# One VectorE instruction for both rows of a sum, and a scratch tile with its channel chunks interleaved by fours

## The chip, the cores and the metric

The kernel runs on one core of a Trainium2 chip. A core has a TensorE (PE) for matrix products, a VectorE (DVE) and a ScalarE (ACT) for elementwise work, a GpSimd (POOL), and a SyncE (SP) that here only issues DMA transfers. The engines run side by side, each through its own list of instructions in order, and wait for each other through semaphores. SBUF is the working memory (128 partitions), PSUM takes what PE writes. The metric is the device time of one execution in microseconds (us), lower is better. Before the change the median of three runs is 2844.78 us (2844.46 to 2845.08).

## The reference

The input `x` has 4 images of 64 channels of 256 x 256 in float32. Four layers follow each other. Layers 0, 1 and 3 are long convolutions with a separable filter per channel (the reference does them by FFT; the filters come from small networks with sines), plus `x * bias`. Layer 2 is the one that the change touches: a two-dimensional Haar transform, two branches that each scale the coefficients, mix the 64 channels and soft-threshold the result, their sum, the inverse transform, and a residual.

```python
f1 = haar2d(x)
acc = jnp.zeros_like(f1[:, :conv_w.shape[1]])
for i in range(v.shape[0]):                       # two branches
    f3 = f1 * v[i]
    f4 = jnp.einsum('bchw,oc->bohw', f3, conv_w[i])
    f5 = jnp.sign(f4) * jax.nn.relu(jnp.abs(f4) - tau[i])
    acc = acc + f5
y = haar2d(acc, inverse=True)
return y + x
```

## The kernel before, in words

**Convolutions** (`convolutions`, `first`, `second`, `contract`). Each image goes channel by channel through layers 0 and 1. A convolution is two products on PE with Toeplitz tiles (L286, L287); ACT copies the first product out of PSUM (L300), VectorE adds the residual to the second (L317). Then VectorE, ACT, POOL and PE do the forward Haar transform: pairs (L366, L367), levels along the row (L379, L380), a split of a number into two parts (L398 on ACT, L403 on VectorE) and a product with a Haar matrix (L410). The coefficients go to DRAM.

**Mixing** (`mixing`, 64 groups `g` per image). A group is two rows of coefficients, with all 64 channels. PE mixes the channels (`mix`, L480): `px` in PSUM holds 16 columns of 64 output channels: two branches, two rows `q`, and two halves of each row with two columns. The products with `v` are made by VectorE for the first `16 - n_act` columns (`scaled`, L502, one instruction per four columns) and by ACT for the others (`scaled_too`, L507). `n_act` is 12 for the first three images and 8 for the last (`N_ACT`), so VectorE has one such instruction per group in the first three mixings and two in the last. ACT then makes the absolute value (`size`, L511) and the sign (`sign`, L514); VectorE subtracts the threshold (`shrink`, L518) and makes max(., 0) times sign (`signed`, L522), 1024 elements each. Last, `add` (L528) sums the two branches into the two rows of `z` to which the group belongs, one instruction of 256 elements per row.

**The tile z.** `z` holds a whole image of the mixed coefficients: 128 partitions with 32,768 numbers each, as `[128, 4, 128, 4, 16]`: a chunk `n` of 16 channels, a row `s`, four column parts `x`, and the channel `c` within the chunk. A row's place is given by `slot`, in such a way that each later step of the inverse transform works in place.

**Inverse** (`inverse`). The inverse Haar transform down the rows is done in `z` on VectorE, by `halve`: `odd = even - odd` (L326) and `even = 2 * even - odd` (L329). `butterfly` does it for the first rows; `level(n, chunk, begin, count)` does it for `count` pairs of rows of one chunk (64 elements per row, 4 column parts by 16 channels). For n of 1, 2, 4, 8, 16, 32 and 64 these have up to 16 pairs at a time, so up to 1024 elements. Then, channel by channel, ACT copies one channel out of `z` (`fetch`, L569: 128 rows by 4 column parts, 512 elements far apart), PE applies the other direction (`rows`, L576 and L577; `halves` and `cols` for some channels), VectorE joins it with the residual (L598, L601, L602), and layer 3 follows as the convolutions did. A part of the channels of the first three images (`put_off`) has its layer 3 in the last mixing (`convolution`).

**Order.** Every step is entered with a time of its own (`at`, in units of one channel or group, from `PLACE` and `LATE`), and the steps are emitted in order of these times; a scheduler then settles each engine's list. The convolutions of the next image lie beside the mixing of the one before it. The first filters, their tables and a few constants are put into `z` before it is used (`room`, `part`).

Of the kernel before, what the change touches and what calls it, by code (L numbers as in the profile page):

```python
# [9 lines left out]
F32 = mybir.dt.float32  # L10
F32R = mybir.dt.float32r
AF = mybir.ActivationFunctionType
ALU = mybir.AluOpType
# [3 lines left out]
B, C, S, EMB, ORD = 4, 64, 256, 33, 64  # L17
P = 128
# [92 lines left out]
def conv_seq_kernel(ctx, tc, x, fz, fw, bias, decay, haar, haar_row, factors, vt, taut, wmix, out):  # L111
# [14 lines left out]
    nc = tc.nc  # L126
# [5 lines left out]
    zpool = ctx.enter_context(tc.tile_pool(name="zpool", bufs=1))  # L132
# [13 lines left out]
    bsb = const.tile([P, 3, C], F32, name="bsb")  # L146


    z = zpool.tile([P, 4, P, 4, 16], F32, name="z")

    sd = zpool.tile([P, 8, 2, 2, P], F32, name="sd")
    sums = zpool.tile([P, 4, 2, P], F32, name="sums")
# [6 lines left out]

    room = z.rearrange("p n s x c -> p (n s x c)")
    free = [0]

    def part(n, parts=P):
# [158 lines left out]
    def halve(even, odd, stay=False):  # L324

        first = nc.vector.tensor_sub(odd, even, odd)  # L326
        if stay and behind[0] is not None:
            tc.add_manual_dep(first.ins, behind[0].ins.name, order, reason="not ahead of the joins")
        nc.vector.scalar_tensor_tensor(even, even, 2.0, odd, ALU.mult, ALU.subtract)  # L329

    def level(n, chunk, begin=0, count=None, stay=False):

        count = n if count is None else count
        v = z.rearrange("p n s x c -> p n s (x c)")[:, chunk].rearrange("p (j e s) x -> p j e s x", e=2, s=P // 2 // n)
        halve(v[:, begin : begin + count, 0, 0, :], v[:, begin : begin + count, 1, 0, :], stay)

    def butterfly():

        v = z.rearrange("p n s (k h) c -> p n s k h c", k=2)
        for h in range(2):  # L340
            halve(v[:, :, 0, 0, h, :], v[:, :, 0, 1, h, :])

# [3 lines left out]
    def at(time, run, unit):  # L348
        events.append((time, len(events), run, unit))
# [104 lines left out]
    def mixing(b, start, n_act):  # L454

        st = {}

        def load(g):
            f = mx.tile([P, 2, S], F32, name=f"f_{b}_{g}", tag="f", bufs=3)
            nc.sync.dma_start(f, coef[b].rearrange("k c p w -> (k c) p w")[:, 2 * g : 2 * g + 2])  # L460
            st[g] = {"f": f}
            if g % GT == 0:
                t = mx.tile([P, 2, GT, 16], F32, name=f"vt_{b}_{g}", tag="vt")
                nc.sync.dma_start(t, scales[:, g // GT])
                st["vt", g // GT] = t

        def scale(g, i):
            return st["vt", g // GT][:, i, g % GT, :]

        def over(g, i, n):  # L470
            return scale(g, i)[:, :n].unsqueeze(2).to_broadcast([P, n, C])

        def mix(g):
            f = st[g]["f"]
            ps = psx.tile([P, 2, 2, S], F32, name=f"px_{b}_{g}", tag="mix")
            for q in range(2):
                for h in range(2):
                    for r in range(2):
                        half = slice(r * C, (r + 1) * C)
                        nc.tensor.matmul(  # L480
                            ps[:, r, q, h * P : (h + 1) * P],
                            f[half, q, h * P : (h + 1) * P],
                            wb[half],
                            start=True,
                            stop=True,
                        )
            if g == 0:

                one, two = ps[:, 0, 0], ps[:, 1, 0]
                d = mx.tile([P, S], F32, name=f"d_{b}", tag="mag")  # L490
                nc.vector.tensor_copy(d, two)
                nc.vector.tensor_sub(two, one, d)
                nc.vector.tensor_add(one, one, d)
            st[g]["f4"] = mx.tile([P, 16, C], F32, name=f"f4_{b}_{g}", tag="f4")
            st[g]["px"] = ps.rearrange("p r q (h i o) -> p r q (h i) o", h=2, i=2)

        def scaled(g):
            px, n = st[g]["px"], 16 - n_act
            for r in range(n // 4):
                j = slice(4 * r, 4 * r + 4)  # L500
                v = scale(g, 0)[:, j].unsqueeze(2).to_broadcast([P, 4, C])
                nc.vector.tensor_tensor(st[g]["f4"][:, j], px[:, r, 0], v, ALU.mult)  # L502

        def scaled_too(g, half):
            px, f4 = st[g]["px"], st[g]["f4"]
            for j in range(16 - n_act + half * (n_act // 2), 16 - (1 - half) * (n_act - n_act // 2)):
                nc.scalar.mul(f4[:, j], px[:, j // 4 % 2, j // 8, j % 4], scale(g, 0)[:, j : j + 1])  # L507

        def size(g):
            mag = st[g]["mag"] = mx.tile([P, 16, C], F32, name=f"mag_{b}_{g}", tag="mag")  # L510
            nc.scalar.activation(mag, st[g]["f4"], AF.Abs)  # L511

        def sign(g):
            nc.scalar.activation(st[g]["f4"], st[g]["f4"], AF.Sign)  # L514

        def shrink(g):
            mag = st[g]["mag"]
            nc.vector.tensor_sub(mag, mag, over(g, 1, 16))  # L518

        def signed(g):  # L520
            mag = st[g]["mag"]
            nc.vector.scalar_tensor_tensor(mag, mag, 0.0, st[g]["f4"], ALU.max, ALU.mult)  # L522

        def add(g):
            parts = st.pop(g)["mag"].rearrange("p (q x i) (n c) -> p q i x n c", q=2, i=2, n=4)
            for q in range(2):
                to = slot(2 * g + q)
                nc.vector.tensor_add(  # L528
                    z[:, :, to].rearrange("p n x c -> p x n c"), parts[:, q, 0], parts[:, q, 1]
                )  # L530


        for g in range(S // 4):
            for name, stage in zip(
                ("mix load", "mix", "scaled", "scaled too", "scaled rest", "size", "sign", "shrink", "signed", "add"),
                (
                    load,
                    mix,
                    scaled,
                    lambda g: scaled_too(g, 0),  # L540
                    lambda g: scaled_too(g, 1),
                    size,
                    sign,
                    shrink,
                    signed,
                    add,
                ),
            ):
                at(start + g + PLACE[name if b + 1 < B else "l " + name], stage, g)

    def inverse(b, start, put_off):

        st = {}
# [11 lines left out]

        def fetch(c):
            a = mx.tile([P, 2, 2, P], F32, name=f"zc_{b}_{c}", tag="mag")
            v = z[:, c // 16, :, :, c % 16].rearrange("p i (k h) -> p h k i", k=2)
            nc.scalar.copy(a, v)  # L569
            st[c]["z"] = a  # L570

# [38 lines left out]
        def when(tick, n, chunk, *span, stay=False):  # L610
            at(tick + PLACE["level"], lambda _: level(n, chunk, *span, stay=stay), 0)

        at(along + 11 + PLACE["level"], lambda _: butterfly(), 0)
        for chunk in range(1, 4):
            turn = start + 16 * (chunk - 1)
# [14 lines left out]
        for c in range(C):  # L630
            for name, stage in zip(("sooner", "early", "fetch", "rows"), (sooner, early, fetch, rows)):
                at(start + c + PLACE[name], stage, c)
            turn = start + c
            if c < 16:
                at(start + c + PLACE["halves"], halves, c)
                at(start + c + PLACE["cols"], cols, c)
                turn += 1
            at(turn + PLACE["join"], join, c)
            if c in put_off:
                at(turn + PLACE["aside"], aside, c)  # L640
            else:
                shift = (0.0, 0.0)
                if put_off and not {c - 1, c + 1}.issubset(put_off):
                    shift = ((-0.27, -0.342), (0.23, 0.158))[c % 3]
                for name, stage in zip(("a3", "a3 copy", "y3", "y3 sum", "out"), last(b, st)):
                    at(turn + PLACE[name] + shift[name[0] != "a"], stage, c)
# [80 lines left out]
def slot(i):  # L727

    if i == 0:
        return 0  # L730
    n = 1 << i.bit_length() - 1
    return (2 * (i - n) + 1) * (P // 2 // n)
# [104 lines left out]
```

## Time and profile before

The profile is one execution, taken by the hardware profiler. Its span runs from the first to the last instruction; the time of that same execution is a little longer.

| | |
|---|---|
| time, median of 3 runs | 2844.78 us |
| time of the profiled execution | 2842.56 us |
| span of the profiled execution | 2840.7 us |
| PE busy | 2732.7 us (96%), 18642 products |
| PE loading weights | 2438.6 us (86%) |
| VectorE busy | 2494.6 us (88%), 4333 instructions |
| ACT busy | 2077.6 us (73%), 4941 instructions |
| POOL busy | 333.9 us (12%) |
| DMA | 653.20 MB, 230 GB/s |

The page also shows the span in 40 equal slices of 71 us; each digit is the share of a slice in which the engine was busy, in tenths. The clock that TensorE was granted (PEclk) was full throughout.

```profile
PE   9999999999999999999999999999999999899999
DVE  5655558999998979999998879999998889999985
ACT  2333348999986559989886658999985669998554
```

The first six slices are the convolutions of the first image. The four mixings are the stretches in which ACT is at eight or nine; an inverse follows each of them.

### The profile page before, as it was taken

To read this page: it belongs to the slowest core of one execution; us is meant where nothing else is said; L and a number is where in the kernel's file an instruction comes from. 1 tells how busy PE (TensorE), PEld (TensorE's weight loads), DVE (VectorE), ACT (ScalarE), POOL (GpSimd) and SP (SyncE) were. 2 spreads that over 40 slices of the span, in tenths; PEclk is the share of its full clock that TensorE was granted. 3 is DMA by queue.
4 is the path that set the end of the run, shared out by engine and by line. 5 is a ranking of instruction groups with operands and counts; after the bars stand their busy time and mean duration, and the time that the engine had idled before them with its cause. 6 is when DMAs were issued, how large, how long until landed. Compare 5 with 4: busy or idle time off the path is not lost. (4 is left out here: it accounts for less than half of the span.)

```text
span 2840.7 us, 56683 instructions
## 1 busy us (share of the span) xinstructions
PE 2732.7 (96%) x18642; PEld 2438.6 (86%) x18642; DVE 2494.6 (88%) x4333; ACT 2077.6 (73%) x4941; POOL 333.9 (12%) x644
## 2 busy tenths in 40 slices
PE   9999999999999999999999999999999999899999
PEld 8999998888889898888889998888889987787998
DVE  5655558999998979999998879999998889999985
ACT  2333348999986559989886658999985669998554
POOL 0111111121111001212210001312210000000000
PEclk9999999999999999999999999999999999999999
DMA  6877787676667886777677986777778988787786
GB/s 200 258 232 231 227 239 220 209 208 208 206 207 251 287 257 203 211 212 209 205 216 246 292 262 201 210 210 214 208 212 241 296 277 249 234 253 228 227 240 200
DMA packets 597209, 653.20 MB, mean 230 GB/s; under 512 B 44625, under 2 KB 513204, under 8 KB 596660
## 3 DMA queue, kind: packets, MB, share of 16 engines
q1 hardware_dynamic: 545460, 599.82, 70.6%
q10 hardware_dynamic: 51456, 49.75, 5.1%
q8 instruction: 150, 2.46, 0.4%
q14 instruction: 143, 1.17, 0.1%
HBM read 428.34 MB, written 221.05 MB: 229 GB/s over the span
## 5 line engine op out<-in xcount | busy, mean ns | idle before, releaser
L286 PE MATMUL py<-t,a 128*128 128x256 f32 x3072 | 946.3, 390 | 48.7 <-ACT a L300 47.7
L300 ACT COPY a<-pa 128x512 f32<-128x512 f32 x768 | 475.1, 619 | 476.6 <-PE pa L287 448.3
L507 ACT ACTIVATE f<-px,vt 128x64 f32<-128x64 f32 x2816 | 607.6, 354 | 104.2 <-DVE f L502 101.9
L287 PEld LDWEIGHTS py<-t,a 128*128 128x128 f32 x3072 | 583.4, 190 | 79.3
L287 PE MATMUL py<-t,a 128*128 128x128 f32 x3072 | 590.0, 274 | 0.0
L286 PEld LDWEIGHTS py<-t,a 128*128 128x128 f32 x3072 | 479.4, 191 | 112.2 <-ACT a L300 74.6
L380 POOL TENSOR_TENSOR sd<-less 128x128 f32<-128x128 f32 (+4 forms) x320 | 188.5, 589 | 1829.7 <-DVE less L379 1498.1
L286 PE MATMUL pa<-t,y 128*128 128x256 f32 x1024 | 316.5, 391 | 45.0 <-DVE y L317 44.2
L569 ACT COPY zc<-z 128x512 f32<-128x512 f32 x256 | 280.8, 1105 | 104.6 <-PE pw L577 96.7
L518 DVE TENSOR_TENSOR mag<-mag,vt 128x1024 f32<-128x1024 f32 x256 | 316.5, 1236 | 7.5 <-ACT mag L511 6.7
L522 DVE SCALAR_TENSOR_TENSOR mag<-mag,f 128x1024 f32<-128x1024 f32 x256 | 317.4, 1240 | 0.9 <-ACT f L514 0.5
L286 PE MATMUL pa<-t,x 128*128 128x256 f32 x1024 | 308.7, 383 | 0.6 <-DMA pad<-z 0.6
L403 DVE TENSOR_TENSOR sp<-sd,sp 128x512 fp32r<-128x512 f32 x256 | 179.3, 700 | 145.7 <-ACT sp L398 144.3
L480 PE MATMUL px<-wb,f 64*128 64x128 f32 x4096 | 303.7, 285 | 2.2 <-ACT f L507 2.2
L511 ACT ACTIVATE mag<-f 128x1024 f32<-128x1024 f32 x256 | 293.9, 1148 | 5.2 <-DVE z L528 1.2
L514 ACT ACTIVATE f<-f 128x1024 f32<-128x1024 f32 x256 | 283.9, 1109 | 4.1
L480 PEld LDWEIGHTS px<-wb,f 64*128 64x128 f32 x4096 | 252.2, 187 | 36.5 <-ACT f L507 3.0
L317 DVE SCALAR_TENSOR_TENSOR y<-x,bsb,py 128x512 f32<-128x512 f32 x256 | 190.3, 743 | 44.0 <-PE py L287 40.6
L286 PE MATMUL pa<-t,u 128*128 128x256 f32 x748 | 224.6, 382 | 0.7 <-PE pw L577 0.7
L287 PEld LDWEIGHTS pa<-t,y 128*128 128x128 f32 x1024 | 194.5, 190 | 26.4
L287 PEld LDWEIGHTS pa<-t,x 128*128 128x128 f32 x1024 | 194.6, 190 | 26.3
L286 PEld LDWEIGHTS pa<-t,y 128*128 128x128 f32 x1024 | 155.6, 191 | 65.3 <-DVE y L317 62.8
(71 smaller groups left out, 4434.6 us busy)
## 6 DMA issues: line engine op xcount, KB each, us to landing
t<-pad SPq DMA_DIRECT2D x767, 256.0 KB, 4.1
x<-in_x SPq DMA_DIRECT2D x256, 256.0 KB, 3.9
coef<-co SPq DMA_DIRECT2D x256, 256.0 KB, 3.2
f<-coef SPq DMA_DIRECT2D x256, 256.0 KB, 3.5
r<-keep SPq DMA_DIRECT2D x256, 256.0 KB, 4.1
out_y<-y ACTq DMA_DIRECT2D x187, 256.0 KB, 4.2
keep<-sums SPq DMA_DIRECT2D x256, 128.0 KB, 2.8
keep<-sd SPq DMA_DIRECT2D x256, 128.0 KB, 2.7
```

The source lines that it names most:

```text
L286: nc.tensor.matmul(ps[:, m, :], src[:, 0, m * P : (m + 1) * P], t[:, ::-1], start=True, stop=False)
L287: nc.tensor.matmul(ps[:, m, P:], src[:, 1, m * P : (m + 1) * P], t[:, : P - 1 : -1], start=False, stop=True)
L300: nc.scalar.copy(a, s["p" + new])
L317: nc.vector.scalar_tensor_tensor(y, s[res], bsb[:, layer, c : c + 1], s["p" + new], ALU.mult, ALU.add)
L380: engine.tensor_tensor(t[:, :, :, half:length], v[..., 0], v[..., 1], ALU.subtract)
L480: nc.tensor.matmul(ps[:, r, q, h * P : (h + 1) * P], f[half, q, h * P : (h + 1) * P], wb[half], start=True, stop=True,)
L507: nc.scalar.mul(f4[:, j], px[:, j // 4 % 2, j // 8, j % 4], scale(g, 0)[:, j : j + 1])
L511: nc.scalar.activation(mag, st[g]["f4"], AF.Abs)
L514: nc.scalar.activation(st[g]["f4"], st[g]["f4"], AF.Sign)
L518: nc.vector.tensor_sub(mag, mag, over(g, 1, 16))
L522: nc.vector.scalar_tensor_tensor(mag, mag, 0.0, st[g]["f4"], ALU.max, ALU.mult)
L569: nc.scalar.copy(a, v)
```

## The change

`z` becomes `[128, 128, 4, 16, 4]`: row `s`, column part `x`, channel `c` within the chunk, and the chunk `n` innermost. A row of all 64 channels is now 256 neighbouring numbers, and the 64 numbers of one chunk in a row are four numbers (16 bytes) apart. The order of the output channels in the mixing weights `wmix` is permuted on the host to match, so that PE delivers the channels in the order `c`, `n`.

With that, `add` writes both rows of a group by one instruction of 512 elements: the two rows are `step` slots apart. In `scaled`, the two instructions of the last mixing become one of 512 elements. `level`, `butterfly` and `fetch` address the new layout: a level reads and writes with a step of four elements, the butterfly works on 64 neighbours, and the fetch steps 256 elements from row to row where it stepped 64.

```diff
-    z = zpool.tile([P, 4, P, 4, 16], F32, name="z")
+    z = zpool.tile([P, P, 4, 16, 4], F32, name="z")
...
-    room = z.rearrange("p n s x c -> p (n s x c)")
+    room = z.rearrange("p s x c n -> p (s x c n)")
...
         count = n if count is None else count
-        v = z.rearrange("p n s x c -> p n s (x c)")[:, chunk].rearrange("p (j e s) x -> p j e s x", e=2, s=P // 2 // n)
+        v = z.rearrange("p s x c n -> p s (x c) n")[:, :, :, chunk]
+        v = v.rearrange("p (j e s) x -> p j e s x", e=2, s=P // 2 // n)
         halve(v[:, begin : begin + count, 0, 0, :], v[:, begin : begin + count, 1, 0, :], stay)
 
     def butterfly():
 
-        v = z.rearrange("p n s (k h) c -> p n s k h c", k=2)
+        v = z[:, 0].rearrange("p (k h) c n -> p k h (c n)", k=2)
         for h in range(2):
-            halve(v[:, :, 0, 0, h, :], v[:, :, 0, 1, h, :])
+            halve(v[:, 0, h], v[:, 1, h])
...
         def scaled(g):
             px, n = st[g]["px"], 16 - n_act
-            for r in range(n // 4):
-                j = slice(4 * r, 4 * r + 4)
-                v = scale(g, 0)[:, j].unsqueeze(2).to_broadcast([P, 4, C])
-                nc.vector.tensor_tensor(st[g]["f4"][:, j], px[:, r, 0], v, ALU.mult)
+            if n == 4:
+                nc.vector.tensor_tensor(st[g]["f4"][:, :4], px[:, 0, 0], over(g, 0, 4), ALU.mult)
+            else:
+                f4 = st[g]["f4"][:, :8].rearrange("p (r j) o -> p r j o", r=2)
+                v = scale(g, 0)[:, :8].rearrange("p (r j) -> p r j", r=2).unsqueeze(3).to_broadcast([P, 2, 4, C])
+                nc.vector.tensor_tensor(f4, px[:, :, 0], v, ALU.mult)
...
         def add(g):
-            parts = st.pop(g)["mag"].rearrange("p (q x i) (n c) -> p q i x n c", q=2, i=2, n=4)
-            for q in range(2):
-                to = slot(2 * g + q)
-                nc.vector.tensor_add(
-                    z[:, :, to].rearrange("p n x c -> p x n c"), parts[:, q, 0], parts[:, q, 1]
-                )
+            parts = st.pop(g)["mag"].rearrange("p (q x i) o -> p q x i o", q=2, i=2)
+            to, step = slot(2 * g), slot(2 * g + 1) - slot(2 * g)
+            v = z.rearrange("p s x c n -> p s x (c n)")[:, to : to + step + 1 : step]
+            nc.vector.tensor_add(v, parts[:, :, :, 0], parts[:, :, :, 1])
...
         def fetch(c):
             a = mx.tile([P, 2, 2, P], F32, name=f"zc_{b}_{c}", tag="mag")
-            v = z[:, c // 16, :, :, c % 16].rearrange("p i (k h) -> p h k i", k=2)
+            v = z[:, :, :, c % 16, c // 16].rearrange("p i (k h) -> p h k i", k=2)
             nc.scalar.copy(a, v)
             st[c]["z"] = a
...
-        "wmix": lay(g["L2_conv_conv_w"].transpose(2, 0, 1).reshape(C, 2 * C)),
+        "wmix": lay(g["L2_conv_conv_w"].transpose(2, 0, 1).reshape(C, 2, 4, 16).swapaxes(2, 3).reshape(C, 2 * C)),
```

## The prediction

> **What bounds the kernel now.** I read the busy time in 40 slices first, then the same by stage for each engine, then the groups of instructions kept apart by shape, the list of waits, and the order of time inside two mixing groups. The stretches below show PE (with its weight loads), VectorE (DVE), ACT and POOL: one of the first convolutions, one each of a mixing, the inverse after it, the last mixing, and the last inverse.
>
> ```profile
> core 0: us, PE busy (x) PEld busy (x) DVE busy (x) ACT busy (x) POOL busy (x), PEclk, DMA share, GB/s
> 284.10:355.10 71.00, 71.00 (x426) 64.83 (x425) 41.66 (x76) 27.18 (x51) 9.24 (x30) 1.00 0.77 228
> ...
> 710.20:781.20 71.00, 66.47 (x480) 57.98 (x479) 70.32 (x112) 66.70 (x194) 11.25 (x20) 1.00 0.68 206
> ...
> 923.20:994.20 71.00, 70.06 (x463) 63.86 (x463) 66.48 (x130) 42.27 (x53) 0.00 (x0) 1.00 0.90 287
> ...
> 2414.60:2485.60 71.00, 63.20 (x518) 54.78 (x519) 71.00 (x117) 68.78 (x179) 0.00 (x0) 1.00 0.78 234
> ...
> 2627.60:2698.70 71.10, 70.45 (x456) 64.99 (x455) 70.33 (x118) 37.50 (x50) 0.00 (x0) 1.00 0.75 227
> ```
>
> The bound changes by stage. The convolutions and most of an inverse are PE's (71.00 of 71; 70.06). The four mixings (about 440 to 852, 1065 to 1491, 1704 to 2130, 2343 to 2600 us) are VectorE's: 70.32 and 71.00 of 71, while PE idles 4 to 8 us per slice. In the last inverse, up to about 2740 us, both are full. PE's 96% over the whole span hides this. VectorE time in a mixing therefore counts nearly one for one.
>
> The groups that the change touches, and those that price it (mean ns of one in the last column before the bar's idle time):
>
> ```profile
> line engine op names shapes xcount | busy us, mean ns | idle before us <-releasers
> L569 ACT COPY zc<-z 128x512 f32<-128x512 f32 x256 | 280.8, 1105 | 104.6 <-PE pw L577 96.7 <-DVE z L528 2.3
> L528 DVE TENSOR_TENSOR z<-mag 128x256 f32<-128x256 f32 x512 | 205.5, 439 | 0.8
> L398 ACT CAST sp<-sd 128x512 fp32r<-128x512 f32 x256 | 178.3, 696 | 4.2 <-POOL sd L380 4.2
> L502 DVE TENSOR_TENSOR f<-px,vt 128x256 f32<-128x256 f32 x320 | 132.1, 441 | 0.1
> L366 DVE TENSOR_TENSOR sums<-y 128x256 f32<-128x256 f32 x256 | 108.2, 423 | 3.5
> L326 DVE TENSOR_TENSOR z<-z 128x1024 f32<-128x1024 f32 x69 | 84.2, 1225 | 0.3
> L326 DVE TENSOR_TENSOR z<-z 128x512 f32<-128x512 f32 x42 | 28.6, 686 | 0.0
> ```
>
> In order of time, one stretch of VectorE in the first mixing (start, length):
>
> ```profile
> 643.23 0.41 DVE L528 TENSOR_TENSOR z<-mag 128x256 f32<-128x256 f32 x1
> 643.57 0.41 DVE L366 TENSOR_TENSOR sums<-y 128x256 f32<-128x256 f32 x1
> 643.90 0.43 DVE L367 TENSOR_TENSOR sd<-y 128x256 f32<-128x256 f32 x1
> ...
> 647.20 0.68 DVE L403 TENSOR_TENSOR sp<-sd,sp 128x512 fp32r<-128x512 f32 x1
> 647.80 0.75 DVE L528 TENSOR_TENSOR z<-mag 128x256 f32<-128x256 f32 x2
> 648.47 0.74 DVE L317 SCALAR_TENSOR_TENSOR y<-y,bsb,py 128x512 f32<-128x512 f32 x1
> ```
>
> Neighbours overlap, so what an instruction takes from its engine is the distance between starts: 0.34 us for 256 elements (643.23 to 643.57), 0.60 for 512 (647.20 to 647.80), 0.67 for two of 256 (647.80 to 648.47).
>
> **What it removes.** The sums of L528 fall from 512 instructions of 256 to 256 of 512: 256 x (0.67 - 0.60) = 17.9 us. The products of L502 in the last mixing fall from 128 to 64: the nearest 512-wide product from PSUM takes 685 ns (L584), as L403's 700, so 64 x 0.07 = 4.5 us; if it took L317's 0.66 between starts, nothing. Per mixing that is 4.5, 4.5, 4.5 and 9.0 us, all where VectorE is full. In the last mixing ACT is next: 68.78 of 71, so at most 3% of 257 us, 7.6, comes through. Gain: 13.5 + 7.6 = 21 us (14 to 22).
>
> [...]
>
> **What it adds.** No instruction; but the halving steps of `level` (L326 and L329) now read both inputs and write in place with a step of four elements (16 bytes), where 64 neighbours lay side by side. The trace has no such VectorE row. Two rows bound it. Below: a step of two (L366 reads, L601 writes) takes 423 and 423 ns against 421 for L326's unstepped 256, so 0 per element. Above: ACT's copy L569 reads this same z with a step of 64 elements and takes 1105 ns, the plain 512-wide L398 696: 0.80 ns more per element. ACT's plain step is 0.81 (L514's 1109 for 1024 less 696, over 512), so its cost per element doubles. VectorE's plain step is (1225 - 686)/512 = 1.05 ns; doubled, 1.05 more. A gain is excluded, since no row with a step is faster than one without. I take the doubling: in a step of two only one side of the instruction was stepped and each element kept a near neighbour, while L569 is the one row with larger steps, on this very tile, and it pays in full. I keep 0 and 0.80 for the other cases.
>
> [...]
>
> Elements per line of code, from the counts by shape in each stretch (69 of 1024, 42 of 512, and 12 each of 256, 128 and 64, the 8 of the butterfly left out): 97,536; two lines at 1.05 ns give 205 us. By stretch: the first three mixings 15,168, 20,288 and 20,288 elements = 31.9, 42.6 and 42.6 us; the last mixing 2,176 = 4.6; the inverses 9,216, 4,096, 4,096 and 22,208 = 19.4, 8.6, 8.6 and 46.6.
>
> **What of it reaches the end.** Mixings: VectorE idles some 4 us in each from its second slice on (0.2 to 1.1 per slice); 3 each may be swallowed: 117.1 - 9 = 108, and 4.6 in the last, which has no idle time. First inverse: its levels lie in 920 to 980 us, where VectorE has 1.2 us idle and PE none to spare later; it can run behind by about a step of 3.3 us (213 us for 64 channels): of 19.4 I take 12 (0 to 18). Second and third: 8.6 against 5.5 idle in the 60 us around: 3 each (0 to 8). Last inverse: 46.6 from 2600 to 2740, where VectorE idles 2.2 us; less a step of lag, 40 (30 to 45); the PE-bound tail after it can't catch up. Queued behind a slower level on VectorE are the products L502 that ACT's L507 waits for, the sums y of L317 that PE's next product waits for (already 44.2 us of PE's idle time), and the joins.
> Sum: 108 + 4.6 + 12 + 6 + 40 = 171; less 21: +150 us.
>
> **At nothing.** The fetch L569 steps 256 elements instead of 64: both far apart; were it to double again (256 x 0.41 = 105 us) ACT, with 5 us or more of each 20 idle in the inverses, would cover most. The butterfly moves from runs of 16 to plain ones, 221 ns either way. The weights' columns are permuted on the host. In the built program the fetches keep their number of waits on VectorE and ACT, levels wait for VectorE alone as before, and the orders of PE, ACT and SP differ by a handful of neighbours; so no new wait between engines, no DMA moved past another. A merged sum gives the first of its two rows 0.27 us later; that is VectorE's own next work.
>
> **Rivals.** (A) The step costs VectorE nothing, like L366's: only the gain, 2844.8 - 21 = 2824 us, faster. For it: steps of 8 bytes are free here; L569 is another engine. Against: L569. (B) The price is ACT's 0.80 ns: 156 us in all; mixings 89.3 - 9 = 80 and 3.5, inverses 8 + 2 + 30, less 21: +103, or 2948; if the inverses hide all theirs at the full price, 108 + 4.6 - 21 = +92, 2936. Against the latter: both engines are full to 2740 us. (C) Two stepped inputs and a stepped output each pay: 410 us on VectorE, of which by the same shares 342 reach the end, less 21: 3166; no row speaks for it. (D) The gain and a small price cancel: at 0.13 ns per element (21/171 of 1.05) the change turns from gain to loss.
>
> **Numbers.** The profiled execution took 2842.56 us (span 2840.7, 1.9 around it), the median is 2844.78, 2.2 above. Forecast: 2844.8 + 150 = 2995, own range 2955 to 3030 (the bounds above and a merge gain of 14 to 22). Chances: forecast 0.60, B 0.18, A 0.17, C 0.03, D 0.02. The range runs from B to the forecast's upper end, 2900 to 3030, and leaves out A, C and D. A measurement tells 0.2% (6 us) from no change: faster 0.17, same 0.02, slower 0.81.
>
> **What would show it.** L326 at 1024 elements near 2.3 us (1.23 under A, 2.05 under B); the merged sum near 0.69 and 256 of them; L502 at 512 wide near 0.69; VectorE over 99% in the mixings, with these some 30 to 40 us longer each; PE's waits on L317 grown; the last inverse some 40 us longer. Wrong above all if L326 keeps 1225 ns, or if VectorE's time grows by 180 us and the span by far less.

## The result, and the profile after

The changed kernel takes 2982.55 us (median of 4 runs, 2980.48 to 2985.22) against 2844.63 us: slower by 138 us, a ratio of 1.0485 (95% interval 1.0472 to 1.0497). Its profiled execution took 2982.83 us with a span of 2981.0 us, 140 more than before.

First four of the five stages shown before, by engine (columns: the stretch and its length, then the busy time of PE, weight loads, VectorE, ACT and POOL, with the number of instructions). The changed kernel, busy time in 40 slices' width:

```profile
core 0: us, PE busy (x) PEld busy (x) DVE busy (x) ACT busy (x) POOL busy (x), PEclk, DMA share, GB/s
...
710.20:781.20 71.00, 61.88 (x442) 53.01 (x442) 70.86 (x98) 62.37 (x185) 13.24 (x20) 1.00 0.66 193
...
923.20:994.20 71.00, 65.66 (x414) 58.37 (x414) 67.05 (x116) 41.32 (x55) 0.00 (x0) 1.00 0.83 259
...
2556.60:2627.60 71.00, 62.10 (x502) 53.86 (x503) 71.00 (x84) 68.24 (x182) 0.00 (x0) 1.00 0.79 233
...
2769.70:2840.70 71.00, 60.78 (x365) 51.83 (x364) 71.00 (x92) 29.22 (x38) 0.00 (x0) 1.00 0.63 188
```

In the mixing VectorE was full before (70.32 of 71 us) and is full now (70.86), with fewer instructions in a slice (98 for 112), and PE's busy time in it falls from 66.47 to 61.88 us. The inverse was PE's (70.06 of 71); now PE has only 65.66, and in the last inverse 60.78 where it had 70.45: PE waits for VectorE there. The wait itself stands in the page's row of the products that read y, first before, then after (us busy, mean ns, idle time before them and who ended it): PE's wait for the sums y of L317 went from 44.2 to 96.7 us.

```profile
L286 PE MATMUL pa<-t,y 128*128 128x256 f32 x1024 | 316.5, 391 | 45.0 <-DVE y L317 44.2
```

```profile
L286 PE MATMUL pa<-t,y 128*128 128x256 f32 x1024 | 322.5, 397 | 97.5 <-DVE y L317 96.7
```

The groups of the changed kernel, shapes apart (mean ns of one after the busy time). The lines moved by a few: the sum L528 is L531, the products are L501 (256 wide) and L505 (512 wide), the fetch is L570.

```profile
line engine op names shapes xcount | busy us, mean ns | idle before us <-releasers
L329 DVE SCALAR_TENSOR_TENSOR z<-z 128x1024 f32<-128x1024 f32 x69 | 144.1, 2089 | 0.1
L326 DVE TENSOR_TENSOR z<-z 128x1024 f32<-128x1024 f32 x69 | 143.9, 2092 | 0.4
L326 DVE TENSOR_TENSOR z<-z 128x512 f32<-128x512 f32 x42 | 46.8, 1118 | 0.0
...
L570 ACT COPY zc<-z 128x512 f32<-128x512 f32 x256 | 282.9, 1113 | 105.9 <-PE pw L578 93.1 <-DVE y L317 5.7 <-DVE z L531 1.8
L531 DVE TENSOR_TENSOR z<-mag 128x512 f32<-128x512 f32 x256 | 181.1, 707 | 0.8
L505 DVE TENSOR_TENSOR f<-px,vt 128x512 f32<-128x512 f32 x64 | 47.3, 739 | 0.0
```

A level of 1024 elements takes 2092 ns where it took 1225: 0.85 ns more per element. Over the 97,536 elements of two lines that is 166 us in lengths of instructions. The merged sums take 181.1 us where the single ones took 205.5. Both changes are there; VectorE's busy time, which counts the overlap of neighbours once, grew by 131 us (2494.6 to 2625.2) and the span by 140.

Where the time lies, from the order of time in both traces (first and last sum of a mixing, first and last fetch of an inverse; us from the start):

| until | before | after | grown by | in this stage |
|---|---|---|---|---|
| first sum, image 1 | 448.7 | 449.4 | 0.7 | 0.7 |
| last sum, image 1 | 847.3 | 869.8 | 22.5 | 21.8 (mixing) |
| last fetch, image 1 | 1030.7 | 1067.5 | 36.8 | 14.3 (inverse) |
| last sum, image 2 | 1483.8 | 1550.5 | 66.7 | 29.9 (mixing) |
| last fetch, image 2 | 1673.8 | 1745.3 | 71.5 | 4.8 (inverse) |
| last sum, image 3 | 2126.8 | 2226.2 | 99.4 | 27.9 (mixing) |
| last fetch, image 3 | 2317.0 | 2420.7 | 103.7 | 4.3 (inverse) |
| first fetch, image 4 | 2608.3 | 2724.4 | 116.1 | 12.4 (last mixing) |
| last fetch, image 4 | 2824.9 | 2965.2 | 140.3 | 24.2 (last inverse) |

### The profile page after: what moved, and what is told of

Same layout as the page of the kernel before. It is cut to its first block, busy times and chain, and to the rows that moved or that the text cites. A ratio compares the mean times of both kernels' runs of the same rounds, so it can differ in the third digit from the quotient of the medians.

```text
span 2981.0 us, 56301 instructions
## 1 busy us (share of the span) xinstructions
PE 2766.7 (93%) x18642; PEld 2447.7 (82%) x18642; DVE 2625.2 (88%) x4013; ACT 2086.4 (70%) x4941; POOL 357.8 (12%) x644
## 3 DMA queue, kind: packets, MB, share of 16 engines
q14 instruction: 139, 1.14, 0.1%
## 5 line engine op out<-in xcount | busy, mean ns | idle before, releaser
L300 ACT COPY a<-pa 128x512 f32<-128x512 f32 x768 | 473.5, 617 | 533.1 <-PE pa L287 448.2
L510 ACT ACTIVATE f<-px,vt 128x64 f32<-128x64 f32 x2816 | 609.0, 350 | 181.1 <-DVE f L501 170.8
L381 POOL TENSOR_TENSOR sd<-less 128x128 f32<-128x128 f32 (+4 forms) x320 | 205.5, 642 | 1911.9 <-DVE less L380 1460.6
L286 PE MATMUL pa<-t,y 128*128 128x256 f32 x1024 | 322.5, 397 | 97.5 <-DVE y L317 96.7
L570 ACT COPY zc<-z 128x512 f32<-128x512 f32 x256 | 282.9, 1113 | 105.9 <-PE pw L578 93.1
L517 ACT ACTIVATE f<-f 128x1024 f32<-128x1024 f32 x256 | 282.7, 1104 | 4.7
L317 DVE SCALAR_TENSOR_TENSOR y<-x,bsb,py 128x512 f32<-128x512 f32 x256 | 190.9, 746 | 46.5 <-PE py L287 36.6
```

The source lines that it names most:

```text
L286: nc.tensor.matmul(ps[:, m, :], src[:, 0, m * P : (m + 1) * P], t[:, ::-1], start=True, stop=False)
L300: nc.scalar.copy(a, s["p" + new])
L317: nc.vector.scalar_tensor_tensor(y, s[res], bsb[:, layer, c : c + 1], s["p" + new], ALU.mult, ALU.add)
L381: engine.tensor_tensor(t[:, :, :, half:length], v[..., 0], v[..., 1], ALU.subtract)
```

## The experiments

Two questions: is it the step of four in the levels that costs the time, and what became of the VectorE time that the merged instructions save?

**Plain levels with both merges.** The changed kernel with `z` seen as row, chunk, column part, channel by the levels and the fetch.

```diff
-    z = zpool.tile([P, P, 4, 16, 4], F32, name="z")
+    z = zpool.tile([P, P, 4, 4, 16], F32, name="z")
...
-        v = z.rearrange("p s x c n -> p s (x c) n")[:, :, :, chunk]
+        v = z.rearrange("p s n x c -> p s n (x c)")[:, :, chunk]
```

> The changed kernel with the merged sum and the merged products, but the levels and the fetch see a row as chunk, column part, channel, so that a level's 64 numbers are neighbours again. The merged sum still writes its 256 numbers of a row straight on, so they land in other channels than they belong to: that part of the computation is changed. Theory 1 (the step of four in the levels costs all of it): L326 at 1024 elements back from 2092 to about 1225 ns, and the time falls below the kernel before by the merges' gain, 2844.6 - 21 = 2824 us (2822 to 2832). Theory 2 (the merged sum, the new order of instructions or the waits of the new layout cost it): L326 may recover, but the time stays above 2900 us.

Measured: 2843.14 us against 2845.83 for the kernel before on the same chip, ratio 0.9993 (0.9983 to 1.0002). From its groups by shape:

```profile
L531 DVE TENSOR_TENSOR z<-mag 128x512 f32<-128x512 f32 x256 | 176.3, 688 | 0.8
...
L326 DVE TENSOR_TENSOR z<-z 128x1024 f32<-128x1024 f32 x69 | 83.7, 1219 | 0.4
```

With the step away, L326 is back at 1219 ns and all 138 us are gone: theory 1 holds, theory 2 falls. But the 21 us that the merges were to bring did not come.

**The step alone.** The changed layout, with the sum and the products in two instructions as before.

```diff
-            v = z.rearrange("p s x c n -> p s x (c n)")[:, to : to + step + 1 : step]
-            nc.vector.tensor_add(v, parts[:, :, :, 0], parts[:, :, :, 1])
+            for q in range(2):
+                v = z.rearrange("p s x c n -> p s x (c n)")[:, to + q * step]
+                nc.vector.tensor_add(v, parts[:, q, :, 0], parts[:, q, :, 1])
```

> The changed kernel's layout of z with a step of four in the levels, but the sum and the last mixing's products in two instructions each, as before the change. Theory 1: the step's 166 us of VectorE time (97,536 elements, two lines, 0.85 ns) reach the end nearly whole, without the merges' gain: 2982.5 + 17 to 21 = 3000 to 3004 us. Theory 2: the time falls back to about 2845 us.

Measured: 2982.49 us, ratio 1.0479 (1.0461 to 1.0496): the time of the full change, not 17 to 21 more. The step carries the whole loss, and the merges are worth nothing in this layout too, though VectorE is busy 21 us less with them (2625.2 against 2646.4). The step by itself made VectorE 152 us busier (2646.4 for 2494.6).

**A step of two.** The kernel before with the chunks of `z` interleaved by twos.

```diff
-    z = zpool.tile([P, 4, P, 4, 16], F32, name="z")
+    z = zpool.tile([P, 2, P, 4, 16, 2], F32, name="z")
...
+        v = z.rearrange("p m s x c n -> p m s (x c) n")[:, chunk // 2, :, :, chunk % 2]
```

> The kernel before, with z in two halves and the two chunks of a half interleaved by twos: the levels step two elements (8 bytes) on both inputs and the output; sum and products are those of before. Theory 1a (the price sets in between a step of two and a step of four): L326 at 1024 elements stays at 1225 ns, time 2845 us (2840 to 2850). Theory 1b (the price grows in proportion with the step): a third of the price of a step of four, 0.28 ns per element, L326 near 1515 ns, time near 2895 us.

Measured: 2849.52 us, ratio 1.0014 (1.0005 to 1.0024), and L326 at 1024 elements 1220 ns. A step of two on both inputs and the output costs the instruction nothing: 1a. The price sets in between 8 bytes (1220 ns) and 16 (2092 in the changed kernel). The time is 3.7 us longer all the same; in the trace the first three inverses take 2 to 3 us more each, for a reason that was not looked for.

**Steps by themselves.** A probe with no part of the computation; the lines of code first, then its groups by shape.

```python
nc.vector.tensor_sub(outs[:, 0:512:1], big[:, 0:512:1], big[:, 8192:8704:1])                  # L121, then steps of
                                                   # 2 (L122), 3 (L123), 4 (L124), 6 (L125), 8 (L126), 16 (L127)
nc.vector.tensor_sub(outs[:, 0:2048:4], big[:, 0:512:1], big[:, 8192:8704:1])                 # L128: output alone
nc.vector.tensor_sub(outs[:, 0:512:1], big[:, 0:2048:4], big[:, 8192:8704:1])                 # L129: one input
nc.vector.tensor_sub(outs[:, 0:512:1], big[:, 0:2048:4], big[:, 8192:10240:4])                # L130: both inputs
                                                   # L135: both inputs in pairs of neighbours, every four
nc.scalar.copy(oa[:, 0:512], big[:, 0:512:1])      # L136, then steps of 2 (L137), 3 (L138), 4 (L139), 8, 16 (L141)
```

> Not the computation at all, but a probe: VectorE subtractions of 512 elements in SBUF with a step of 1, 2, 3, 4, 6, 8 and 16 elements on both inputs and the output; a step of 4 on the output alone, on one input alone, on both inputs alone; the two-step form with a scalar at a step of 4 and of 1; 1024 and 2048 elements at a step of 4; pairs of neighbours every four; and ACT copies of 512 with a step of 1, 2, 3, 4, 8 and 16 on the input and of 4 on the output; 16 of each. If the price is for each access to another 16 bytes: flat (700 ns) at 1 and 2, in between at 3, about 1120 ns at 4 and the same at 6, 8 and 16; pairs cost nothing. If it grows with the step: 16 far above 4. If only inputs pay, the output alone stays at 700 ns; if three streams share one path, both inputs alone would cost less than all three. ACT: 696 at 1 and 2, 1105 at 4 and beyond.

```profile
L139 ACT COPY oa<-big 128x512 f32<-128x512 f32 x16 | 17.8, 1115 | 0.5
L124 DVE TENSOR_TENSOR outs<-big 128x512 f32<-128x512 f32 x16 | 17.3, 1084 | 0.5
...
L128 DVE TENSOR_TENSOR outs<-big 128x512 f32<-128x512 f32 x16 | 17.1, 1069 | 0.5
...
L130 DVE TENSOR_TENSOR outs<-big 128x512 f32<-128x512 f32 x16 | 17.1, 1068 | 0.5
L129 DVE TENSOR_TENSOR outs<-big 128x512 f32<-128x512 f32 x16 | 17.1, 1066 | 0.5
L127 DVE TENSOR_TENSOR outs<-big 128x512 f32<-128x512 f32 x16 | 16.7, 1045 | 0.6
...
L123 DVE TENSOR_TENSOR outs<-big 128x512 f32<-128x512 f32 x16 | 13.5, 846 | 0.5
L122 DVE TENSOR_TENSOR outs<-big 128x512 f32<-128x512 f32 x16 | 11.1, 693 | 0.5
...
L135 DVE TENSOR_TENSOR outs<-big 128x512 f32<-128x512 f32 x16 | 11.1, 692 | 0.5
L121 DVE TENSOR_TENSOR outs<-big 128x512 f32<-128x512 f32 x16 | 11.0, 688 | 0.5
L137 ACT COPY oa<-big 128x512 f32<-128x512 f32 x16 | 10.6, 661 | 0.5
L136 ACT COPY oa<-big 128x512 f32<-128x512 f32 x16 | 9.9, 619 | 27.1 <-DVE oa L119 26.6
```

Read down the last-but-one number: 688 ns plain, 693 at a step of two, 846 at three, 1084 at four, and no more at sixteen (1045). One stepped stream out of three pays as much as all three (1066 to 1069), the output as much as an input. Pairs of neighbours every four elements cost nothing (692). So in these rows the full price stands where each element is 16 bytes or more from the one before it (four and sixteen elements), and part of it at 12 bytes; on ACT too the price is there at a step of four (1115 ns for 619 plain, 661 at two). This fits the expectation's first case, a price for each access to another 16 bytes; what in the chip makes it, these rows do not show. The size is (1084 - 688)/512 = 0.77 ns per element on VectorE here, 0.85 by length in the kernel, and (1115 - 619)/512 = 0.97 on ACT.

**The same merges with plain levels, computed in full** (the relaid kernel below). `z` as before; instead the products and thresholded terms are laid out as chunk, column, channel, so that one sum covers both rows.

```diff
-            st[g]["f4"] = mx.tile([P, 16, C], F32, name=f"f4_{b}_{g}", tag="f4")
+            st[g]["f4"] = mx.tile([P, 4, 16, 16], F32, name=f"f4_{b}_{g}", tag="f4")
...
+            parts = st.pop(g)["mag"].rearrange("p n (q x i) c -> p n q x i c", q=2, i=2)
+            to, step = slot(2 * g), slot(2 * g + 1) - slot(2 * g)
+            nc.vector.tensor_add(z[:, :, to : to + step + 1 : step], parts[:, :, :, :, 0], parts[:, :, :, :, 1])
```

> The kernel before with z, levels, butterfly and fetch untouched; the products and the thresholded terms are laid out as chunk, column, channel instead, so that the sum of both rows and the last mixing's products are one instruction each without any step in the levels. ACT's products L507 and VectorE's L502 write runs of 16. Theory 1: L326 at 1225 ns, the sum near 0.70 us for 512, time 2824 us (2820 to 2834), faster than both kernels. Rival: runs of 16 cost ACT time on 2816 products; at 20 ns each 56 us, of which the last mixing, where ACT has 2 us idle of 71, would pay 20: about 2840 to 2850 us.

Measured: 2842.93 us, ratio 0.9991 (0.9982 to 1.0000): no loss, and again hardly a gain. Runs of 16 cost ACT next to nothing (L510 takes 610.9 us in all, against 607.6 before).

**The last mixing's products alone, merged.** The kernel before with that edit of `scaled`.

> The kernel before with one edit: the last mixing's products with v in one instruction of 512 elements instead of two of 256. 64 x 0.07 = 4.5 us less VectorE time in a stage that VectorE bounds, with ACT at 68.8 of 71 behind it: 2840 to 2841 us. If ACT's chain sets the last mixing instead, 2844 to 2845 us. If the wider product delays ACT's start on the group, slower.

Measured: 2848.20 us, ratio 1.0014 (1.0005 to 1.0023): slower, if by little. 3 us less work on VectorE (2491.3 for 2494.6) and 4 us more time. Its last mixing is 4.8 us longer, and the trace shows with what: 8 level instructions of 1024 elements lie in it where the kernel before has 3.

So why do the merges bring nothing? In the last mixing, a group of the kernel before takes 4.26 us; VectorE fills all of it (71.00 of 71 us in the last mixing's stretch of the prediction). With the merges VectorE needs 4.13 (2499.66 to 2503.79 between the same instruction of two groups of the first kernel of this section, plain levels with both merges). ACT in order of time, first a group of the kernel before, then one of that kernel:

```profile
2504.22 1.06 ACT L511 ACTIVATE mag<-f 128x1024 f32<-128x1024 f32 x1
2505.18 0.57 ACT L300 COPY a<-pa 128x512 f32<-128x512 f32 x1
2505.65 1.06 ACT L514 ACTIVATE f<-f 128x1024 f32<-128x1024 f32 x1
2506.62 1.74 ACT L507 ACTIVATE f<-px,vt 128x64 f32<-128x64 f32 x8
2508.48 1.06 ACT L511 ACTIVATE mag<-f 128x1024 f32<-128x1024 f32 x1
```

```profile
2499.61 0.57 ACT L300 COPY a<-pa 128x512 f32<-128x512 f32 x1
2500.07 1.75 ACT L510 ACTIVATE f<-px,vt 128x64 f32<-128x64 f32 x8
2501.85 1.06 ACT L514 ACTIVATE mag<-f 128x1024 f32<-128x1024 f32 x1
2502.94 1.06 ACT L517 ACTIVATE f<-f 128x1024 f32<-128x1024 f32 x1
2503.91 0.57 ACT L300 COPY a<-pa 128x512 f32<-128x512 f32 x1
```

Before, ACT has 0.11 us to spare in 4.26 (from the end of L507 at 2508.36 to 2508.48). With the merges, size and sign stand back to back here (1.09 apart, where the copy between them gives 0.96), and ACT needs 4.30 with no gap. The kernel before has them so too, in 40 of the 64 groups of the last mixing, with the merges in 57. Besides, some 10 us of levels came over from the last inverse into VectorE's free time (four pairs of instructions of 1024 elements and a half, where the kernel before has one and a half), so that VectorE is full as well. Two possible covers of the gain, then, lie over each other; the next runs take them away, one by one and together.

**Levels held back.** The relaid kernel with the levels of 16 pairs and more of the last image behind its last sum, by a dependency that orders only VectorE's list (`tc.add_manual_dep(first.ins, final[B - 1].ins.name, order, ...)`).

> The relaid kernel (merged sum and products, plain levels), with the last image's levels of 16 pairs and more held behind the last sum, where the kernel before has all but one. Theory F (the freed VectorE time of the last mixing was filled with levels that came in from the last inverse, where nothing is gained by their leaving): some 9 us of levels go out again and the last mixing shortens by about as much, 2834 us. Theory A (ACT sets the last mixing: 4.30 us per group with size and sign back to back, against VectorE's 4.13): VectorE only idles more, 2842 to 2844 us.

Measured: 2849.40 us, ratio 1.0019 (1.0010 to 1.0028): outside both ranges. VectorE idles, as theory A says (busy 37.64 of 40 us near the end of the last mixing), and the mixing is no shorter, while the last inverse has the levels to do. But ACT is not full there either (37.11 of 40), so the trace does not show that ACT sets the pace. The stretch, with the columns of the stages above:

```profile
2560.00:2600.00 40.00, 35.23 (x282) 30.76 (x284) 37.64 (x46) 37.11 (x97) 0.00 (x0) 1.00 0.79 235
```

**The copy between size and sign.** The relaid kernel with ACT's order in the last mixing tied: size, copy of a product, sign (which is entered 0.245 of a group later for it).

> The relaid kernel, with ACT's copy of a product put between size and sign of a group in the last mixing, as the second half of the kernel before has it: 0.96 + 0.47 + 0.97 + 1.75 = 4.15 us per group on ACT instead of 4.30. The levels stay where the scheduler has them. Theory A alone: 64 x 0.13 = 8 us less, 2835 us. If the filling levels hold VectorE at 4.13 + 10/64 = 4.29 us per group: no gain, 2841 to 2844 us.

Measured: 2840.33 us, ratio 0.9988 (0.9979 to 0.9997). It is the fastest version here that computes everything, 3.6 us below the kernel before, not the 8 of theory A. The relaid kernel without this edit was 2.9 us below the kernel before on its own chip, so the copy in between is worth about 1 us, which the spread of the runs does not tell from nothing.

**Both.**

> Both edits: levels held behind the last sum and the copy between size and sign. Theory F and A together (two limits, each hiding the other): ACT 4.15 and VectorE 4.13 per group against 4.27 before, 64 x 0.12 = 7.7 us less in the last mixing, about 2835 us, where each edit alone gives little. If only one of them was the reason, this equals the better of the two alone. If the last inverse has no room for the held levels, no gain: 2843 us or more.

Measured: 2842.78 us, ratio 0.9995 (0.9987 to 1.0004). Neither VectorE (38.2 of 40 us) nor ACT (38.2) is full in the 80 us up to 2600, near the end of the last mixing, and a group there takes 4.42 us (2529.90 to 2534.32 for L538): both are waiting in turn. The trace shows who waits: VectorE's `signed` for ACT's sign, ACT's products for VectorE's, and PE's next `mix` for ACT's products, each for 0.16 to 0.20 us in nearly every group. From the list of waits of these 80 us (us in all, times, longest):

```profile
DVE mag L538 <- ACT f L528: 3.7, 18, 0.2
ACT f L519 <- DVE f L514: 3.1, 18, 0.2
PEld px L489 <- ACT f L519: 2.8, 17, 0.2
```

The time is close to that of the last expectation (no gain), but its reason does not fit: the last inverse grew by only 0.8 us (217.5 for 216.7).

**ACT relieved, without and with the merges.** Half of ACT's sign left out: `AF.Sign` on `f4[:, :8]`, or on half the chunks in the relaid kernel.

> The kernel before, with ACT's sign (L514) left out for half of each group's columns: 512 elements, 0.43 us less ACT work per group, 256 groups; the thresholded terms of those columns lose their sign treatment. VectorE's work is untouched. Theory A (VectorE sets the mixings, with ACT's chain close under it): VectorE stays full and the time stays within 3 us of 2844. If ACT sets the mixings already: up to 256 x 0.43 = 110 us less.

> The relaid kernel (merged sum and products, plain levels) with the same 512 elements of ACT's sign left out per group. Theory A (the merges' 22 us of VectorE time did not come through because ACT's chain stood right behind VectorE): with ACT relieved they come through, 12 to 21 us below the kernel before with the same cut, 2824 to 2833 us. If something else than ACT holds the mixings at their length (PE's products, the transfers), the time stays at 2840 to 2844 us.

Measured, in this order: 2835.53 us, ratio 0.9965 (0.9952 to 0.9979), and 2838.00 us, ratio 0.9974 (0.9963 to 0.9985). ACT is 99 us less busy in the kernel before (1978.8 for 2077.6), and that is worth 9 us of time, more than the 3 expected and far less than 99: VectorE sets most of the mixings, with ACT close by. Of the 9, 6.8 us lie in the first three mixings and about half a us in the last. The merges are worth nothing even so: with them it is 2838.00 against 2835.53. So ACT is not what hides them. VectorE is full in the last mixing of both kernels (40.00 of 40), and the four pairs of levels and a half fill what the merges freed. One stretch of it without the merges, then with them:

```profile
2520.00:2560.00 40.00, 37.14 (x302) 32.21 (x299) 40.00 (x68) 35.60 (x103) 0.00 (x0) 1.00 0.86 250
```

```profile
2520.00:2560.00 40.00, 36.29 (x294) 31.64 (x292) 40.00 (x49) 36.12 (x102) 0.00 (x0) 1.00 0.87 252
```

**Both covers off.**

> The relaid kernel with both covers taken off: 512 elements of ACT's sign left out per group (as in the two runs before this one), and the last image's levels of 16 pairs and more held behind the last sum. In the run with the cut alone VectorE was full in the last mixing (40.00 of 40 us) and carried some 10 us of levels that the kernel before keeps for the last inverse. Theory F+A: with ACT out of the way the levels' leaving now shortens the last mixing by 7 to 10 us, and the last inverse, where PE is full, does not grow by as much: 2828 to 2833 us. Rival: a ring of waits over PE, ACT and VectorE holds the group at 4.3 us whatever is taken off: VectorE idles, 2838 to 2848 us.

Measured: 2841.90 us, ratio 0.9987 (0.9978 to 0.9996), 3.6 us below the kernel before on its own chip where the run before is 6.8 below: no gain, and inside the rival's range. VectorE idles, as the rival says (38.28 to 39.35 of 40 us from 2400 us on). It also has its instructions in another order in some groups. A stretch by engine, then one in order of time:

```profile
2520.00:2560.00 40.00, 35.74 (x291) 31.14 (x290) 39.00 (x47) 34.39 (x100) 0.00 (x0) 1.00 0.82 240
```

```profile
2523.06 1.22 DVE L528 SCALAR_TENSOR_TENSOR mag<-mag,f 128x1024 f32<-128x1024 f32 x1
2524.31 0.69 DVE L533 TENSOR_TENSOR z<-mag 128x512 f32<-128x512 f32 x1
2524.92 0.68 DVE L508 TENSOR_TENSOR f<-px,vt 128x512 f32<-128x512 f32 x1
2525.53 1.22 DVE L524 TENSOR_TENSOR mag<-mag,vt 128x1024 f32<-128x1024 f32 x1
2526.66 0.74 DVE L317 SCALAR_TENSOR_TENSOR y<-v,bsb,py 128x512 f32<-128x512 f32 x1
2527.32 1.22 DVE L528 SCALAR_TENSOR_TENSOR mag<-mag,f 128x1024 f32<-128x1024 f32 x1
```

This group takes 4.26 us again (2523.06 to 2527.32). Here the merged sum stands right behind the instruction whose result it reads: it starts 1.25 us after that, where a next instruction that reads something else starts after 1.13 (2525.53 to 2526.66). The 0.12 us are just about what the two merges save in a group. But only 21 of the 64 sums stand so, 2.5 us in all, and VectorE's idle time in this mixing is 5.1 us more than in the run before (9.5 for 4.4). Later groups take 4.34 and 4.63 us in turn; in the longer ones VectorE waits 0.28 us for ACT's size (L517), and ACT's products wait for VectorE's (10.1 us in the last 80 us before 2600).

The last mixing and the last inverse of each version, from the order of time in its trace (us; level work from start to start, idle time that of VectorE in the mixing):

| version | last mixing | level work in it | VectorE idle in it | last inverse |
|---|---|---|---|---|
| kernel before | 291.2 | 7.6 | 5.2 | 216.7 |
| last products merged alone | 296.0 | 16.0 | 5.6 | 217.4 |
| plain levels, both merges | 293.0 | 18.0 | 5.0 | 217.6 |
| relaid, levels held back | 297.7 | 8.3 | 13.5 | 220.3 |
| relaid, copy between | 292.7 | 16.3 | 6.0 | 216.0 |
| relaid, both | 293.3 | 9.7 | 11.1 | 217.5 |
| relaid, half the sign | 292.4 | 18.1 | 4.4 | 216.2 |
| relaid, half the sign, levels held | 294.0 | 9.5 | 9.5 | 219.2 |

The account of the third row closes: apart from levels and idle time VectorE's work in the last mixing fell from 278.4 to 270.1 us, 8.3 less, which is what the merges were to save; 10.4 us of levels came in, and the mixing is 1.8 us longer. The last inverse lost these 10.4 us of VectorE's work and is no shorter. Where the levels are held back, VectorE's idle time grows by 4 to 8 us instead. So in none of these versions did the last mixing become shorter than before. Why VectorE waits once the levels are held is seen in the traces as waits between ACT, VectorE and PE, and no run took these away; whether the merges can bring their 8 us in the last mixing stays open. In the first three mixings, 0.3, 2.0 and 2.0 us of the 4.5 saved arrive in the kernel with plain levels. VectorE waits more there: in the second, for ACT's split L399 (L398 before), 6.4 us against 3.7. That was seen in the traces and not tried by itself.

## Why the prediction came out as it did

The forecast was 2995 us, the measurement 2982.55. For the step the mechanism was the one forecast; for the merges it was not. Two terms of the sum were mis-sized, the price of the step by 33 us and the gain of the merges by 21, and that these errors go in opposite directions, so that 12 us are left, is luck.

- *What bounds the kernel.* Right: the mixings are VectorE's, and the step's cost shows there first (21.8, 29.9 and 27.9 us in the first three).
- *The price of the step.* Taken as a doubling of VectorE's own 1.05 ns per element, from ACT's copy that doubles ACT's. Measured 0.85 by length, nearer to the 0.80 of rival B: 166 us instead of 205. Lengths count the overlap of neighbours twice, which the prediction itself takes care not to do; by busy time the step alone cost VectorE 152 us, 0.78 per element. In the probe ACT pays 0.97 and VectorE 0.77, so VectorE shares neither ACT's factor nor its price. That L569 was the right row to go by, though it is another engine and a far larger step, the probe shows: between a step of four (1084 ns) and one of sixteen (1045) the step's size hardly matters, and one stepped stream is enough (1066 to 1069).
- *The share that reaches the end.* 171 of 205, 83%, was forecast; the step alone took 137 us (2982.49 less 2845.83). That is 82% of the 166 us of lengths, but 90% of the 152 us by which VectorE became busier: the stages hid less than was forecast.
- *By stage.* Scaled to 0.85 and without the merges, the forecast's mixings give 25.8, 34.5 and 34.5 us of VectorE time; 21.8, 29.9 and 27.9 arrived. The inverses: 14.3 against 12, 4.8 and 4.3 against 3 each. The last mixing and the last inverse, forecast at -3 and +40, came to 12.4 and 24.2. With the step alone they grew by 3.4 and 31.6, close to the forecast's 4.6 and 40 scaled to 0.85 (3.7 and 32.4); with the merges, 18 us of levels by their starts (three pairs of 1024 elements and smaller ones) lie in the last mixing instead of the last inverse.
- *The gain of the merges.* This is the step that failed: 21 us (14 to 22) were to come through because VectorE was full. The durations were right (0.61 us between starts for a merged sum), VectorE's time did fall by 20 us, and next to nothing arrived: 2982.49 and 2982.55 without and with them, and 2.7 us with plain levels (2843.14 against 2845.83), at the edge of what the runs can tell. "ACT is next, at most 3%" took the order of the lists as given, and relieving ACT did not bring the gain out. In the last mixing the lists are new: level work that the kernel before does in the last inverse fills the freed time (18.0 us of it for 7.6) and is not missed where it left. The prediction compared the orders of PE, ACT and SP and said nothing of VectorE's.
- *The sum.* 0.85/1.05 = 0.81, and 171 x 0.81 - 0 = 138.5. The price was 33 us too high, the gain 21 too high; the difference is the 12 us between forecast and result. The bounds written beside the terms would give an own range of 2965 to 3022, narrower than the 2955 to 3030 stated.
- *At nothing.* The fetch, four times farther apart, takes 1113 ns for 1105: right. A merged sum's later first row did not show in the fetches, which wait 1.8 us for the sums where they waited 2.3.
- *Rivals.* A falls with L326 at 2092 ns, and D with it (0.85 is far from 0.13). B had the better price, in part by the row it was read from: L398 at 696 ns turns its numbers into fp32r, and a plain copy takes 619 in the probe, so that ACT's own price is 0.97 and not 0.80. C falls with the probe, where three stepped streams (1084 ns) cost what one does (1066).

## What to carry to other kernels

Before interleaving a tile to make one instruction contiguous, count the elements of every other instruction that reads or writes it: with float32 numbers in SBUF, a step of four elements (16 bytes) cost 0.77 ns more per element on VectorE in the probe and 0.85 in the kernel, and 0.97 on ACT in the probe; on VectorE a step of sixteen cost much the same (1045 ns for 512 elements, against 1084 at four), and pairs of neighbours cost nothing (692 against 688). Where only one side needs another order, change the layout of the small operand that is written anew each time (here the thresholded terms) and leave the large tile that many instructions walk through (2842.93 us, where the interleaved tile took 2982.55). And a saving on an engine that is 99% busy is not yet a saving of time (2982.49 us without the merges, 2982.55 with them): look at what a scheduler will move into the gap, whether it is missed where it came from, and at the waits that are left when nothing fills the gap.

## What the runs showed that was not expected

- One stepped stream of three costs as much as all three (1066, 1069 and 1084 ns for one input, the output and all, against 688), and a step of three costs part of it (846).
- On VectorE the sum that stands right behind the `signed` whose result it reads starts 1.24 to 1.29 us after it in the changed kernel (24 sums), a little more than that instruction's whole length of 1.21 to 1.26; the sums y of L317, which read something else, start 1.13 or 1.14 us after it (123 of 129).
- On ACT, size and sign back to back start mostly 1.09 us apart in the last mixing (33 of 40 in the kernel before), and mostly 1.19 to 1.21 in the first three (84 of 90). A copy from PSUM (L300) starts 0.95 to 0.97 us behind size (109 of 110 in that kernel), and so does the cast of `sd` from SBUF (L398, 13 of 15). The sign also overwrites the tile that size reads; whether that makes the difference was not tried.
- POOL's largest instruction (128 elements) went from 1215 to 1452 ns in the changed kernel, though POOL's own work is unchanged; POOL waits 1.9 ms in all, and little came of it (ACT's split waits 6.9 us for it, 4.2 before). Why it takes longer stays open.
